# Reordering the end of a graph-attention kernel: the last pieces of k, two projection pieces, the statistics and the last row blocks' tiles

## Chip, cores, metric

One Trainium2 chip (trn2), one of its cores. The metric is the time of the whole kernel on the device in microseconds (us); lower is better. The kernel is already tuned: 3693 us long, TensorE busy for 99% of it.

## The reference, cut to what matters

Two layers on x of shape (32, 512, 512). The first is a graph convolution with residual and layer norm. The second is 8-head attention, masked by the adjacency matrix, again with residual and layer norm. There are 32 graphs (the kernel's *batches*) of 512 nodes with 512 features.

```
x = layernorm(x + deg * (x @ Wi.T + b) + adj @ (x @ Wj.T))
q, k, v = x @ Wq.T + bq, x @ Wk.T + bk, x @ Wv.T + bv          # 8 heads of 64
s = where(adj == 0, -inf, q k^T / 8)
x = layernorm(x + softmax(s) v @ Wo.T + bo)
```

## The kernel before: what the change touches

Batches are pipelined. While batch n does its attention in eight steps (scores, masked exponentials, values), TensorE is filled between the steps with *pieces* of other batches' projections: seven products per 512 x 512 block, named 1 to 7, each eight matmuls. `pj` is the output projection (pieces p1 to p7), `k` the key projection (k1 to k7). The last period has few pieces left, and that is where the change is. The list below is the last period; each inner list is one attention step of the last batch.

```
LATE = (5, 3, 6, 7, 4)
ALONE = ((1, "a"), (6, "b"), (2, "a"), (7, "b"), (5, "a"), (4, "b"), (3, "a"))

def phase_a(n):                      # the pieces at the end of a period
    A, K = banks(n)
    if n == B:
        return [pc("k", n - 1, i, bank) for i, bank in ((6, K), (5, A), (7, K), (3, A), (4, K))]
    ...

def last_steps():
    m = B - 2
    p = {i: pc("pj", m, i, bank) for i, bank in ALONE}
    c = [z(combos, TO, m, ot_quarter(m), (1, 2)), z(combos, TO, m, ot_quarter(m), (3, 4))]
    own = [(4 * GA, last_part, c, 0) for c in range(2)]
    return [[z(last_load), FLUSH, c[0], p[1], c[1]], [p[2], p[6]], [p[5], p[7], z(add_bo, B - 1, 0), z(add_bo, B - 1, 1)],
            [p[3], p[4], z(stats, m, 0), z(stats, m, 1)], [z(apply, m, 0), z(apply, m, 1), z(store, m)], [own[0]], [own[1]], []]
```

Words used below, with their lines in the kernel before: the *mask product* (VectorE, L495) multiplies the exponentials by the mask and so frees the scores' PSUM tile; *pre-sums* and *sums of weights* (L501 on GpSimd, L503 on VectorE) add up the weights of a row, and `sums` (L522) makes its *denominators* of them on TensorE; reciprocals (L531) and scalings (L547) turn values into the scaled output oT and so free the values' PSUM tiles `ov`; *combinations* (GpSimd, L405) are sums of blocks of oT that the seven products need, `add_bo` (GpSimd, L387) the additions of the output bias; a *final unit* is a pair of matmuls of the last batch's output projection (`last_part`, L735 and L736); *statistics* (L298) are those of the layer norm, and the ScalarE pass that follows them at the end is L743. A step is *bare* when no piece stands in it. `FLUSH` issues at once all that is left of `rest`. (In later kernels the line numbers are a few lower or higher.)

The loop that runs a step: scores first, then the values of the step before, at the start of a group of four also its denominators (`sums`) and what follows from them (`rest`: four reciprocals, two scalings, one check sum), then the pieces, with the pre-sums of the weights (`presum`) and the rest dealt out between them.

```
scores(b, 2 * g, kc); scores(b, 2 * g + 1, kc)
values(pb, pg, pk)
if pk == NC - 1:
    sums(pg, ...); drain(pb, pg); extra = rest(pb, pg)
late = [(presum, i, kc) for i in range(2) if kc > 0]
for f in PERIODS[n][step]:
    if f is FLUSH: some = len(extra)
    else:
        run(f)
        some = 0 if f[0] == 0.0 else len(extra) if step == 0 else max(1, round(f[0] / PC))
    if some:
        for g in late[:1] + extra[:some]: g[0](*g[1:])
        late, extra = late[1:], extra[some:]
for g in late + extra: g[0](*g[1:])
```

And the tail. `sc_tile()` gives a two-bank PSUM tile, of which there are two; `RL[g]` holds the denominators, as (PSUM tile, SBUF tile).

```
    else:
        t = sc_tile()
        ACC[2], ACC[3] = t[:, 0, :], t[:, 1, :]        # in last_part: two row blocks in one tile
...
for c in range(2):
    last_part(c, 1)
for ic in range(NC):
    c = slice(ic * P, (ic + 1) * P)
    invert(1, ic, 0)                                     # reciprocal straight from PSUM
    scale(B - 1, 1, 0, c); scale(B - 1, 1, 1, c)
    last_part(2, ic=ic); last_part(3, ic=ic)
    if ic > 0: last_rows(ic - 1)                         # BN statistics, ScalarE pass, store
tell_all(B - 1, 1)
last_rows(NC - 1)
flags()
```

## Time and profile before

| | before |
|---|---|
| time | 3696.01 us, median of 3 (3695.45 to 3696.68) |
| profiled execution | span 3693.0 us, granted clock 0.998 |
| TensorE busy | 3662.9 us, 99% |
| VectorE, GpSimd, ScalarE busy | 65%, 53%, 28% |

The page and the views that matter are shown in the prediction below. In a timeline line, read: start and length in us, engine, source line, operation, output <- input, number of instructions merged; in brackets the idle time before the line and what ended it. In a windows line: the stretch and its length; busy time and instructions of PE, PEld, DVE, ACT, POOL; then granted clock, DMA share, GB/s.

### The profile page before, as it was taken

What the parts mean: (1) busy time and instruction counts of PE and PEld (TensorE: products, weight loads), DVE (VectorE), ACT (ScalarE), POOL (GpSimd) and SP (SyncE); (2) the same over time, 40 slices, a digit from 0 to 9 for tenths busy, and PEclk for the clock granted to TensorE, in tenths of its full rate; (3) what the DMA queues carried; (4) which work ended last, traced back from release to release, by engine and by line L of the source; (5) the groups of instructions that cost most, each with busy time, mean ns of one, the idle gap of its engine ahead of it and who ended that gap; (6) DMA issues with size and microseconds to landing.
All of it is one profiled execution on the core that took longest, in us unless ns stands there. A gap on an engine that the chain in (4) does not pass through costs nothing.

```text
span 3693.0 us, 49640 instructions
## 1 busy us (share of the span) xinstructions
PE 3662.9 (99%) x18470; PEld 2510.3 (68%) x18470; DVE 2393.1 (65%) x3134; ACT 1028.6 (28%) x1483; POOL 1940.0 (53%) x1985
## 2 busy tenths in 40 slices
PE   9999999999999999999999999999999999999998
PEld 6766667676767676767676767676767666666663
DVE  4666666666666666666666666666666666666665
ACT  2232232222222223222223222223232322222322
POOL 3555545556445555455554555644555545555443
PEclk9999999999999999999999999999999999999999
DMA  8445556444555445564555544455545555445541
GB/s 258 141 120 140 138 154 160 139 131 135 151 157 151 129 135 146 152 165 125 135 140 151 162 144 128 136 150 155 158 123 138 142 158 159 134 133 139 148 138 44
DMA packets 797173, 530.02 MB, mean 144 GB/s; under 512 B 530432, under 2 KB 611840, under 8 KB 796928
## 3 DMA queue, kind: packets, MB, share of 16 engines
q1 hardware_dynamic: 780384, 494.78, 49.7%
q10 hardware_dynamic: 16320, 31.46, 2.3%
q8 instruction: 151, 2.47, 0.3%
q14 instruction: 94, 0.77, 0.1%
q0 software_dynamic: 224, 0.53, 0.0%
HBM read 453.25 MB, written 73.40 MB: 143 GB/s over the span
## 4 chain that ended last, share of the span: by engine, by line
PE 97%; DVE 1%; POOL 0%; DMA 0%; ACT 0%; SPq 0%; issue 0%; DVEq 0%; ACTq 0%; POOLq 0%
PE mma L436 31%; PE mmb L436 31%; PE sc L490 13%; PE ov L512 12%; PE mmb L334 4%; PE mma L334 3%; PE sc L522 2%; PE mmb L611 0%; PE mma L611 0%; DVE e L495 0%; DVE rl L531 0%; DMA xa<-hd 0%; SPq L376 0%; PE sc L736 0%; DVE st L298 0%
## 5 line engine op out<-in xcount | busy, mean ns | idle before, releaser
L494 ACT ACTIVATE sc<-sc 128x1024 f32<-128x1024 f32 x512 | 493.0, 1007 | 1554.8 <-PE sc L490 1548.8
L495 DVE TENSOR_TENSOR e<-sc,edge 128x1024 f32<-128x1024 f32 x512 | 602.6, 1218 | 205.8 <-ACT sc L494 173.3
L436 PE MATMUL mmb<-ring,big 128*128 128x256 f32 x3144 | 731.7, 381 | 0.0
L436 PE MATMUL mma<-ring,big 128*128 128x256 f32 x3112 | 724.4, 381 | 1.5 <-DVE xh L454 0.8
L436 PEld LDWEIGHTS mmb<-ring,big 128*128 128x128 f32 x3144 | 591.9, 190 | 131.6 <-issue 27.7
L436 PEld LDWEIGHTS mma<-ring,big 128*128 128x128 f32 x3112 | 585.8, 190 | 132.3 <-issue 26.5
L405 POOL TENSOR_TENSOR big<-big 128x512 f32<-128x512 f32 x376 | 492.4, 1339 | 34.5 <-DVE big L382 14.3
L490 PE MATMUL sc<-q,k 64*128 64x512 f32 x2048 | 509.4, 615 | 0.0
L512 PE MATMUL ov<-e,v 128*32 128x512 f32 x4096 | 492.4, 598 | 4.6 <-DVE oT L547 4.6
L501 POOL TENSOR_TENSOR es<-e 128x1024 f32<-128x1024 f32 x128 | 300.8, 2361 | 350.2 <-DVE e L495 350.2
L436 PE MATMUL mma<-big,ring 128*128 128x256 f32 x1808 | 430.3, 381 | 0.0
L436 PE MATMUL mmb<-big,ring 128*128 128x256 f32 x1776 | 422.8, 381 | 1.0 <-DVE v L465 1.0
L300 POOL TENSOR_SCALAR mv<-mv 128x1 f32<-128x1 f32 x256 | 49.8, 194 | 674.2 <-DVE mv L299 661.9
L436 PEld LDWEIGHTS mma<-big,ring 128*128 128x128 f32 x1808 | 340.5, 190 | 73.0 <-issue 26.0
L436 PEld LDWEIGHTS mmb<-big,ring 128*128 128x128 f32 x1776 | 334.3, 190 | 73.4 <-issue 26.0
L512 PEld LDWEIGHTS ov<-e,v 128*32 128x32 f32 x4096 | 106.9, 109 | 351.9 <-issue 320.8
L204 POOL TENSOR_TENSOR xlo<-xh,xhi 128x512 fp32r<-128x512 f32 x128 | 162.7, 1283 | 338.1 <-ACT xhi L203 338.1
L490 PEld LDWEIGHTS sc<-q,k 64*128 64x128 f32 x2048 | 176.3, 186 | 208.2 <-issue 207.0
L349 POOL TENSOR_TENSOR big<-big,deg_r 128x512 f32<-128x512 f32 x124 | 173.5, 1400 | 263.5 <-DVE big L348 263.5
L503 DVE TENSOR_TENSOR es<-es,e 128x1024 f32<-128x1024 f32 x250 | 304.8, 1220 | 0.0
L454 DVE TENSOR_TENSOR xh<-xh,mma 128x512 f32<-128x512 f32 x186 | 126.7, 681 | 263.9 <-PE mma L436 263.9
L454 DVE TENSOR_TENSOR xh<-xh,mmb 128x512 f32<-128x512 f32 x186 | 126.7, 681 | 259.2 <-PE mmb L436 259.2
(161 smaller groups left out, 3663.6 us busy)
## 6 DMA issues: line engine op xcount, KB each, us to landing
ring<-wo SPq DMA_DIRECT2D x217, 256.0 KB, 2.8
ring<-wq SPq DMA_DIRECT2D x160, 256.0 KB, 3.9
ring<-wv SPq DMA_DIRECT2D x160, 256.0 KB, 3.4
ring<-wk SPq DMA_DIRECT2D x160, 256.0 KB, 3.3
ring<-wi SPq DMA_DIRECT2D x155, 256.0 KB, 2.7
ring<-wj SPq DMA_DIRECT2D x155, 256.0 KB, 2.6
xh<-in_x_dram SPq DMA_DIRECT2D x32, 1024.0 KB, 5.4
xa<-in_x_dram SPq DMA_DIRECT2D x124, 256.0 KB, 4.0
```

The source lines that it names most:

```text
L204: nc.gpsimd.tensor_sub(lo, xs, hi.bitcast(FT))
L334: nc.tensor.matmul(pm, parts[w][:, jc, :], adjR[:, jc, :], start=(w == 0 and jc == 0), stop=(w == 1 and jc == NC - 1))
L349: nc.gpsimd.tensor_tensor(XD[b][:, dc, :], XD[b][:, dc, :], deg_r, op=OP.mult)
L405: nc.gpsimd.tensor_tensor(dst, p, q, op=OP.subtract)
L436: nc.tensor.matmul(pm[:, c * Q:(c + 1) * Q], lhs, rhs, start=first, stop=(kc == 1 and n == len(terms) - 1), skip_group_check=True)
L454: nc.vector.tensor_tensor(d, d, pm, op=OP.add)
L490: nc.tensor.matmul(ps[:, s, :], KT[b, hp // 2][r, hp % 2, kc * P:(kc + 1) * P], QT[b, hp // 2][r, hp % 2, :], start=True, stop=True)
L494: nc.scalar.activation(ps, ps, AF.Exp, scale=QSCALE)
L495: nc.vector.tensor_tensor(e, ps, edge[:, kc:kc + 1, :].to_broadcast([P, 2, N]), op=OP.mult)
L501: nc.gpsimd.tensor_add(ES[i], E[i, 0], E[i, 1])
L503: nc.vector.tensor_add(ES[i], ES[i], E[i, kc])
L512: nc.tensor.matmul(PV[g][r][32 * h:32 * h + 32, :], V[b][:, kc, c0:c0 + 32], E[h // 2, kc][:, h % 2, :], start=(kc == 0), stop=(kc == NC - 1))
```

## The change

Two of k's last five pieces go behind the last batch's first scores; p3 and p4 go behind the first denominators of the last batch; the statistics of the batch before come later still; the last two row blocks get a tile each; and the last denominators are drained into SBUF as all others are.

```diff
@@ phase_a
-            return [pc("k", n - 1, i, bank) for i, bank in ((6, K), (5, A), (7, K), (3, A), (4, K))]
+            return [pc("k", n - 1, i, bank) for i, bank in ((5, A), (6, K), (3, A))]
@@ last_steps
-        p = {i: pc("pj", m, i, bank) for i, bank in ALONE}
+        A, K = banks(B)
+        p = {i: pc("pj", m, i, K if i in (6, 7, 4) else A) for i in ORDER}
...
-        return [[z(last_load), FLUSH, c[0], p[1], c[1]], [p[2], p[6]], [p[5], p[7], z(add_bo, B - 1, 0), z(add_bo, B - 1, 1)],
-                [p[3], p[4], z(stats, m, 0), z(stats, m, 1)], [z(apply, m, 0), z(apply, m, 1), z(store, m)], [own[0]], [own[1]], []]
+        k = [pc("k", B - 1, i, K) for i in (7, 4)]
+        return [[z(last_load), k[0], FLUSH, c[0], p[1], c[1], k[1]], [p[2], p[6]], [p[5], p[7], z(add_bo, B - 1, 0), z(add_bo, B - 1, 1)],
+                [], [p[3], p[4]], [own[0], z(stats, m, 0), z(stats, m, 1)], [own[1], z(apply, m, 0), z(apply, m, 1), z(store, m)], []]
@@ last_part
-                t = sc_tile()
-                ACC[2], ACC[3] = t[:, 0, :], t[:, 1, :]
+                ACC[ic] = sc_tile()[:, 0, :]
@@ the tail
-    for c in range(2):
-        last_part(c, 1)
+    drain(B - 1, 1)
     for ic in range(NC):
         c = slice(ic * P, (ic + 1) * P)
-        invert(1, ic, 0)
+        invert(1, ic)
         scale(B - 1, 1, 0, c)
         scale(B - 1, 1, 1, c)
+        if ic < 2:
+            last_part(0, 1, ic + 2)
+            last_part(1, 1, ic + 2)
         last_part(2, ic=ic)
         last_part(3, ic=ic)
...
-    tell_all(B - 1, 1)
+    tell(B - 1, 1)
```

More of the change, by code (lines that the diff above doesn't have):

```diff
@@ L527, in drain, with invert @@
         nc.scalar.activation(RL[g][1], RL[g][0], AF.Identity, accum_out=told[:, j:j + 1])
-    def invert(g, part, src=1):
+    def invert(g, part):
         c = slice(part * P, (part + 1) * P)
-        nc.vector.reciprocal(RL[g][1][:, c], RL[g][src][:, c])
+        nc.vector.reciprocal(RL[g][1][:, c], RL[g][1][:, c])
     def tell(b, g):
@@ L535, in tell @@
         nc.vector.reduce_sum(told[:, j:j + 1], RL.pop(g)[1], axis=AX.X)
-    def tell_all(b, g):
-        pl, rl = RL.pop(g)
-        j = 2 * (b * 2 + g)
-        nc.gpsimd.memset(told[:, j + 1:j + 2], 0.0)
-        nc.vector.tensor_tensor_reduce(pl, pl, rl, 1.0, 0.0, OP.add, OP.add, told[:, j:j + 1])
     def scale(b, g, r, c=slice(0, N)):
@@ L568, in gnn_attention_kernel @@
     LATE = (5, 3, 6, 7, 4)
-    ALONE = ((1, "a"), (6, "b"), (2, "a"), (7, "b"), (5, "a"), (4, "b"), (3, "a"))
     def banks(n):
```

## The prediction

> **What bounds the kernel now.** I read the page first, then TensorE's timeline over the last 200 us, the windows with the granted clock, the chain of waits over the same stretch, and the timelines of VectorE and GpSimd beside it.
>
> ```profile
> PE 3662.9 (99%) x18470; PEld 2510.3 (68%) x18470; DVE 2393.1 (65%) x3134; ACT 1028.6 (28%) x1483; POOL 1940.0 (53%) x1985
> ```
>
> TensorE is busy for 99% of 3693.0 us; its idle time lies mostly in the first 15 us and in the end. The change keeps every matrix product (the built kernels have the same number of matmuls) and first departs from the kernel before at 3567 us. So only the last 126 us can change, and within them TensorE's gaps and the tail after its last product. The gaps (last bracket of a line: idle before it, and who ended it):
>
> ```profile
> 3571.61 1.92 PE L512 MATMUL ov<-e,v 128*32 128x512 f32 x16 [0.63 <-DVE oT L547]
> 3590.77 1.99 PE L436 MATMUL mmb<-big,ring 128*128 128x256 f32 x8 [0.98 <-DVE v L465]
> 3613.29 1.92 PE L512 MATMUL ov<-e,v 128*32 128x512 f32 x16 [1.18 <-DVE oT L547]
> 3639.74 1.50 PE L522 MATMUL sc<-es,ones 128*32 128x512 f32 x8 [2.00 <-DVE e L495]
> 3641.00 1.95 PE L522 MATMUL sc<-e,ones 128*32 128x512 f32 x8
> 3642.88 2.35 PE L490 MATMUL sc<-q,k 64*128 64x512 f32 x8
> 3647.96 1.92 PE L512 MATMUL ov<-e,v 128*32 128x512 f32 x16 [2.73 <-DVE oT L547]
> 3676.50 1.98 PE L736 MATMUL sc<-xh,oT 128*128 128x512 f32 x4 [0.46 <-DVE oT L547]
> 3678.69 1.98 PE L736 MATMUL sc<-xh,oT 128*128 128x512 f32 x4 [0.20 <-DVE oT L547]
> ```
>
> The two denominator lines (L522) last 1.50 and 1.95 us where the same eight take 1.04 elsewhere. The windows view says why: its clock column, after POOL's, falls to 0.56 just after the 2.00 us gap and is back at 1.00 four us later.
>
> ```profile
> 3638.00:3640.00 2.00, 0.26 (x4) 0.16 (x8) 1.97 (x4) 0.00 (x0) 1.63 (x5) 1.00 0.00 0
> 3640.00:3642.00 2.00, 2.00 (x16) 0.38 (x8) 0.82 (x1) 0.00 (x0) 1.02 (x4) 0.56 0.00 0
> 3642.00:3644.00 2.00, 2.00 (x12) 0.70 (x6) 0.28 (x1) 1.00 (x3) 0.00 (x0) 0.59 0.04 8
> 3644.00:3648.00 4.00, 1.26 (x10) 0.23 (x8) 3.90 (x6) 4.00 (x6) 0.00 (x0) 1.00 0.14 51
> ```
>
> The chain at the very end (start, us, what): the last statistics stand behind ScalarE's pass over the block before.
>
> ```profile
> 3680.71 0.71 DVE st L298
> ...
> 3682.94 0.78 ACT xh L743
> 3683.74 0.71 DVE st L298
> ...
> 3685.97 0.78 ACT xh L743
> ```
>
> The waits of the built code agree: that last BN-stats waits for ScalarE, because both blocks sit in one two-bank tile.
>
> **What the Trainium skill says.** "TensorE: Matmul & The Clock Gate", Part 1, has the clock fall to half after about one idle window of 3.4 us, and a window that runs freely. The trace agrees on the half rate (0.56) and the length, but 2.00 us of idle was enough; the 2.73 us gap brought none. "PSUM — Partial Sum Buffer", PSUM bank collisions, forbids two engines on one bank and allows different banks; the two halves of an sc tile are two banks, so separate tiles may drop that last wait. No collision shows here. "SBUF — State Buffer", Who interferes with whom, says a VectorE instruction with two SBUF inputs contends with GpSimd's reads. The trace agrees: the sums of weights (L503) take 1.22 us alone and 1.77 beside GpSimd's bias additions (L387).
>
> **The change, part by part.** I measure losses from start to start. Natural steps, from the timeline: a piece of eight products 1.73 us, 0.1 more beside a score step; scores 1.92; values 1.85; denominators 0.86 for eight; a final unit of two 0.86.
>
> *k's last pieces.* One piece fewer stands before the scores at 3569, so these start at 3567.26 and their values could at 3569.18. VectorE frees the old ov tiles: reciprocals from 3567.98 (four at 0.85, one already done) end at 3569.77, and values begin 0.74 after the first scaling starts, at 3570.52. Loss 1.34 instead of 0.70: +0.64. Next, the v piece and k piece that shared bank b back to back are parted by scores: the loss at 3590.77 (2.87 from start to start, less 1.73 = 1.14) goes. Three pieces, k7, p1, k4, now follow the denominators. From 3570.52 I add 1.86, two groups of 10.87 (four pieces, scores, values), 9.14 (three), 0.97, 5.38 and 1.92: values at 3611.5. The first scaling starts at 3606.1+0.65 (a k addition)+3.4 (reciprocals) = 3610.15, so they are free at 3610.9; the loss of 1.25 goes. Balance against 3613.29: -1.8.
>
> *The pieces p3 and p4 behind the denominators.* The kernel before has 12.93 from those values to the scores of the fourth step: 3624.43 now. Their values end at 3628.2, and nothing stands between them and the next scores, whose tile is free only after VectorE's mask product. That hangs on GpSimd: combinations from 3611.6, 7.39 to the presums, 4.69 to the second mask product, 5.65 to the first of the next pair: 3629.3, finished 3630.5. A **new wait** of 2.35 us, and 0.2 for the second half. Then values 3632.7, denominators 3634.5 (no statistics ahead of them: the 2.07 and the slow 1.42 go), p3 3636.25, p4 3638.1, scores 3639.9. VectorE: p4's addition at 3640.1, three reciprocals 2.6, scaling 3643.35, values at 3644.1. Loss 2.28 instead of 3.16. Against 3647.96: -3.9, if the clock holds.
>
> *Statistics after the next scores.* They leave the denominators' path, but GpSimd's twelve small operations (four times 1.27 us) now stand between its two presums. First presum 3646.45 to 3648.8; small ones to 3653.9; second presum to 3656.3. The mask product of the next step reuses the block that it reads, ends at 3657.5, and the second half of the last scores waits for it: 1.27 lost. At the first final unit: 3667.20-3.9+1.3 = 3664.6, -2.6.
>
> *Row blocks' tiles and denominators through SBUF.* The drain on ScalarE puts about 0.7 us ahead of the first reciprocal, but three units lie beside it: that reciprocal at 3665.4, its scaling usable at 3666.85, TensorE gets there at 3667.25. The fourth scaling, behind the second block's statistics as before, lets the last group begin at 3675.7 instead of 3678.69: -3.0. The 0.68 us reduction replaces a custom operation of 0.81. Last statistics: 2.02 after that group's start, 3677.7, against 3683.74. ScalarE no longer in front is a further -3.0. The tail from there is unchanged, the memset aside.
>
> Sum: -3.0 - 3.0 = -6.0 us, span 3687.0, time 3690.0. Then the clock. A half-rate window costs about 1.7 us. With gaps of 1.7 us harmless and 2.0 harmful, the free window catches the new 2.35 us gap in about half the runs and the 2.28 us one nearly so: an estimate of 1.5 us in the mean. **Prediction: 3691.5 us, -0.12%.**
>
> **Rivals.** (1) *The ends simply add, no new wait*: all six gaps vanish, 10 us, plus 3 at the tail: 3683. Against it: GpSimd's presums already hold a mask product for 4.08 us in this trace, and the pieces that covered it are moved. (2) *Bare steps starve TensorE twice*: scores, values, scores, values, denominators are light, both gaps fall to half clock, the late presum costs 2 us more: 3694 to 3697, no gain. For it: one 2 us gap did this before. (3) *The tail is set by something else* (the flag or the last store): then the last 3 us stay, 3693 to 3694.5. Against: the last ScalarE pass ends at 3686.75 and the span 6.25 later; the flag's last operation ends 0.8 before it, and in the new order the flag follows the same statistics, so all move together.
>
> **Range and chances.** Low 3687.5: no half-rate window and waits 2.5 us smaller than my walk. High 3696: rival 2 nearly whole, or a chip that sits a little higher; three runs before spread over 1.2 us. A gain or loss of 2% would be 74 us, half the stretch concerned: faster 0.003, slower 0.007, same 0.99.
>
> **What would show it.** Right: no idle before the products near 3590 and 3613; a new wait of about 2.3 us ahead of scores near 3630, ended by VectorE's e; about 2.3 us ahead of values near 3644, ended by oT; a GpSimd presum at about 3654, after small operations, and about 1.3 us before scores near 3657; the last statistics on VectorE ended by TensorE, not ScalarE; last final group at about 3676. Wrong: half clock in none or both places moves the end by 1.7 us each; a last wait on the flag or a store refutes the tail; movement before 3567 us would mean that something outside the diff differs.

## The result

| | before | after |
|---|---|---|
| median, lowest to highest, us | 3695.4, 3692.25 to 3696.68 (6 runs) | 3690.06, 3688.87 to 3691.26 (6 runs) |
| ratio, 95% interval | | 0.9987, 0.9974 to 1.0 |
| profiled span | 3693.0 | 3687.9 |

A ratio here is the mean time of one kernel's fast runs over the mean of the other's of the same rounds, so not quite the ratio of the medians quoted. The verdict at 2% is "same", as foreseen: 5.3 us of 3695. The time lies in the range; the middle was 1.4 us too high.

TensorE's timeline after, the lines with an idle time and, unbracketed, the values that follow the second of them (compare the nine lines of before in the prediction):

```profile
3570.41 1.92 PE L512 MATMUL ov<-e,v 128*32 128x512 f32 x16 [1.26 <-DVE oT L540]
...
3630.51 3.46 PE L490 MATMUL sc<-q,k 64*128 64x512 f32 x8 [2.42 <-DVE e L495]
3633.91 2.09 PE L512 MATMUL ov<-e,v 128*32 128x512 f32 x16
...
3645.35 1.92 PE L512 MATMUL ov<-e,v 128*32 128x512 f32 x16 [2.08 <-DVE oT L540]
...
3658.76 1.13 PE L490 MATMUL sc<-q,k 64*128 64x512 f32 x4 [1.10 <-DVE e L495]
...
3676.98 1.98 PE L730 MATMUL sc<-xh,oT 128*128 128x512 f32 x4 [0.46 <-DVE oT L540]
```

The waits near 3590 and 3613 are gone. The first has grown (1.26), a new one stands at 3630, the one for the scaled outputs has shrunk from 2.73 to 2.08, and half of the last scores waits 1.10. The scores at 3630 last 3.46 us where eight such matmuls take 1.99. The windows view after gives the reason, in its clock column (0.72, 0.50, 0.93):

```profile
3630.00:3632.00 2.00, 1.49 (x4) 0.59 (x6) 1.59 (x2) 0.00 (x0) 0.45 (x1) 0.72 0.00 0
3632.00:3634.00 2.00, 2.00 (x10) 0.44 (x10) 0.65 (x1) 1.01 (x1) 0.00 (x0) 0.50 0.00 0
3634.00:3636.00 2.00, 2.00 (x20) 0.59 (x24) 1.52 (x2) 1.01 (x1) 0.00 (x0) 0.93 0.00 0
...
3682.00:3684.00 2.00, 0.00 (x0) 0.00 (x0) 0.00 (x0) 0.00 (x1) 0.00 (x0) 0.52 0.43 132
```

(The last line lies behind the last product. It costs nothing, but dates the clock's windows further down.)

GpSimd's timeline after: its two pre-sums (L501), with twelve small operations between them, of which the first is shown.

```profile
3647.70 2.35 POOL L501 TENSOR_TENSOR es<-e 128x1024 f32<-128x1024 f32 x1 [17.25 <-DVE e L495]
3650.13 0.19 POOL L300 TENSOR_SCALAR mv<-mv 128x1 f32<-128x1 f32 x1
...
3655.09 2.35 POOL L501 TENSOR_TENSOR es<-e 128x1024 f32<-128x1024 f32 x1
```

VectorE's timeline after: the mask product that waited for that second pre-sum (TensorE's 1.10 us hang on it), and the last statistics, now released by TensorE and not by ScalarE.

```profile
3657.48 2.49 DVE L495 TENSOR_TENSOR e<-sc,edge 128x1024 f32<-128x1024 f32 x2 [3.13 <-POOL es L501]
...
3679.01 0.70 DVE L298 BATCH_NORM_STATS2 st<-sc 128x6 f32<-128x512 f32 x1 [0.49 <-PE sc L730]
```

**A common zero.** Single executions differ by more than these effects, before the change begins: the denominators of batch after batch keep nearly the same distances in the traces compared (58.2 and 55.2 us in turn; from the first of them to the *zero* defined next 3397.8 to 3398.5 us), but the first starts at 160.2 us in one and 164.2 in another, though the kernels are the same up to there. Most of the difference lies in the first microseconds: waits for the adjacency matrix, and products at half speed (the first four of 128x512, L193, last 2.07 us before and 1.21 in "pre-sums first"; the clock column shows 1.00 there all the same). So I measure within a trace, from the start of the last denominators (L522) ahead of the change, those of the first group of the last batch but one, called *zero* (3560.91 us before, 3560.81 after). The marks: the values that run in step 1 of the last period; the first values after the last batch's first denominators (those of step 4; they run in step 5); the first final unit; the last ScalarE pass. Each mark comes from one profiled execution per kernel. The expectations below call the zero "the seventh (batch's last) denominators" and the last batch "the eighth"; these are slips, their 105.15 us is counted from this zero. "Half" counts stretches of half clock before the last product.

| kernel | time, us | values step 1 | values step 4 | first final unit | last ScalarE pass | half |
|---|---|---|---|---|---|---|
| before | 3695.40 | 52.38 | 87.05 | 106.29 | 125.06 | 1 |
| after | 3690.06 | 50.51 | 84.54 | 105.15 | 120.42 | 1 |
| tail only | 3689.99 | 52.38 | 86.68 | 107.50 | 122.77 | 2 |
| order only | 3693.40 | 50.51 | 84.55 | 105.17 | 123.95 | 1 |
| k's pieces only | 3692.17 | 50.50 | 83.40 | 103.98 | 122.76 | 1 |
| after, statistics at once | 3693.51 | 50.51 | 87.98 | 108.85 | 124.13 | 2 |
| after, pre-sums first | 3689.14 | 50.50 | 84.59 | 104.28 | 119.54 | 1 |
| after, reciprocals first | 3689.62 | 50.51 | 82.41 | 103.74 | 119.01 | 1 |
| after, p1's additions first | 3686.23 | 50.50 | 81.33 | 101.95 | 117.21 | 0 |
| after, these three | 3684.21 | 50.50 | 79.20 | 99.62 | 114.88 | 0 |
| k's pieces and tail | 3689.64 | 50.51 | 83.40 | 104.28 | 119.55 | 1 |
| after, bias early | 3687.18 | 50.51 | 82.15 | 102.75 | 118.02 | 0 |
| after, p3 back | 3687.05 | 50.51 | 82.27 | 103.15 | 118.42 | 1 |
| after, four edits | 3683.84 | 50.51 | 78.26 | 98.69 | 113.96 | 0 |

Times are medians: six runs each for the first two rows, five for the others. The kernel before, run again beside the others, had medians of 3694.1, 3694.36 and 3693.62 us (9 runs in each of the three groups). Where two kernels differ by about a microsecond, only the marks tell them apart.

### The profile page after: what moved, and what is told of

Its sections match the earlier page's. It is cut to its first block, busy times and chain, and to the rows that moved or that the text cites. A ratio compares the mean times of both kernels' runs of the same rounds, so it can differ in the third digit from the quotient of the medians.

```text
span 3687.9 us, 49638 instructions
## 1 busy us (share of the span) xinstructions
PE 3662.2 (99%) x18470; PEld 2511.0 (68%) x18470; DVE 2393.1 (65%) x3133; ACT 1029.4 (28%) x1485; POOL 1939.0 (53%) x1984
## 4 chain that ended last, share of the span: by engine, by line
PE 98%; DVE 1%; POOL 1%; ACT 0%; issue 0%; DMA 0%; SPq 0%; DVEq 0%; POOLq 0%; ACTq 0%
PE mma L436 31%; PE mmb L436 31%; PE sc L490 13%; PE ov L512 13%; PE mmb L334 4%; PE mma L334 3%; PE sc L522 2%; PE mmb L604 0%; PE mma L604 0%; POOL es L501 0%; DVE e L495 0%; DVE rl L531 0%; PE sc L730 0%; DMA big<-in_adj_dram 0%; POOL big L405 0%
## 5 line engine op out<-in xcount | busy, mean ns | idle before, releaser
L501 POOL TENSOR_TENSOR es<-e 128x1024 f32<-128x1024 f32 x128 | 300.1, 2355 | 363.5 <-DVE e L495 363.5
```

The source lines that it names most:

```text
L501: nc.gpsimd.tensor_add(ES[i], E[i, 0], E[i, 1])
```

## The experiments

All gave the reference's result. My theory: the gain is a sum of separate waits, -1.8 (k's pieces), a small loss or gain from moving p3, p4 and the statistics, and -3.5 (tail). Rivals: the tail is set by something else; the reordering does everything; later waits absorb what earlier ones give.

### Tail only

The kernel before, with the last two parts of the diff (a tile for each row block, and the tail) alone.

> The kernel before with only the new tail: the last denominators drained by ScalarE into SBUF, a tile for each of the last two row blocks, their products in the new order. Theory (the tail is worth what its own chain shows, whatever comes before): 3.0 us because the last statistics no longer wait for ScalarE, 0.3 to 0.6 more from the order of the final units; 3.3 to 3.8 us faster than before, the two gaps near 3640 and 3648 unchanged. Rival (the tail gains only because TensorE arrives earlier, or the flag sets the end): under 1 us.

3689.99 us, ratio 0.999 (0.9976 to 1.0003). From the first final unit to the last ScalarE pass: 15.27 us (122.77 - 107.50) against 18.77 before (125.06 - 106.29): **-3.50**, with 15.27 in the changed kernel as well. VectorE's timeline of this run, its last statistics:

```profile
3679.66 0.70 DVE L298 BATCH_NORM_STATS2 st<-sc 128x6 f32<-128x512 f32 x1 [0.49 <-PE sc L735]
```

It waits for TensorE alone. That the tile of its own frees it, and not the drain or the new order in the same edit, is read from who ended the wait (ScalarE before, TensorE here); no run parts the three. From the start of the last final group to these statistics there are 2.02 us (3679.66 - 3677.64) against 5.05 before (3683.74 - 3678.69), so 3.0 of the 3.5 are the wait for ScalarE. The rival falls. The second gap is 2.37 us and not 2.73 as expected, because the scores ahead of it last longer at half clock (2.70 us, 2.35 before). This trace also caught two stretches of half clock, one more than before, which is why its first final unit comes later (107.50) though nothing ahead of it was touched. TensorE's timeline of this run, the second of them: values that take 3.50 us and not 1.92.

```profile
3645.80 3.50 PE L512 MATMUL ov<-e,v 128*32 128x512 f32 x16 [2.37 <-DVE oT L547]
```

### Order only

The kernel before, with `phase_a` and `last_steps` of the change alone.

> The kernel before with only the new order of pieces and statistics, the old tail. Theory (the parts add): what is left of the change after the tail, 1.2 us with one half-rate window as in the trace of after, 2.6 us without one; a new wait near 3630, a late second presum on GpSimd at about 3655. Rival (the order gives everything, the tail is hidden): 4 us or more. Rival (the order gives nothing, new waits eat all): within 0.5 us.

3693.40 us, ratio 0.9999 (0.9986 to 1.0013). First final unit at 105.17, **-1.12** against before, one stretch of half clock in both, and the three new waits as in the changed kernel (2.41, 2.08 and 1.11 us). Order -1.12 and tail -3.50 make -4.62; the changed kernel has -4.64 (125.06 - 120.42). The parts add.

### k's pieces only

```diff
-                [], [p[3], p[4]], [own[0], z(stats, m, 0), z(stats, m, 1)], [own[1], z(apply, m, 0), z(apply, m, 1), z(store, m)], []]
+                [p[3], p[4], z(stats, m, 0), z(stats, m, 1)], [z(apply, m, 0), z(apply, m, 1), z(store, m)], [own[0]], [own[1]], []]
```

(`last_steps` of the change with p3, p4 and the statistics where they had been; the tail of before.)

> The kernel before with only k's last two pieces moved behind the denominators; the projection's p3 and p4 and the statistics stay where they were. Theory: -1.8 us at the values near 3613 (the waits of 0.98 and 1.18 gone, the one near 3571 0.7 larger), carried to the end since the later waits hang on GpSimd and VectorE work that starts about 2 us earlier as well: 1.8 to 2.4 us faster. Rival (later waits absorb it, being fixed by other work): under 0.7 us at the end.

3692.17 us, ratio 0.9996 (0.9982 to 1.0009). Values of step 1 at 50.50 (-1.88), first final unit at 103.98: **-2.31**, and 1.19 us *earlier* than with the whole new order. So moving p3, p4 and the statistics costs 1.2 us in this pair of traces. TensorE's timeline of this run shows what it would have replaced:

```profile
3636.30 1.06 PE L522 MATMUL sc<-es,ones 128*32 128x512 f32 x8 [1.75 <-DVE e L495]
...
3643.26 3.28 PE L512 MATMUL ov<-e,v 128*32 128x512 f32 x16 [3.09 <-DVE oT L547]
```

Two waits, 4.84 us together, and one half-clock stretch; in the changed kernel three, 2.42, 2.08 and 1.10, 5.60 together, and one half-clock stretch. The move trades waits at a small loss.

### k's pieces and tail

The changed kernel with the same edit.

> The change without what its words name last: k's pieces and the tail as changed, but p3 and p4 ahead of the denominators and the statistics behind them as in the kernel before. Theory (from the two parts measured alone: -2.2 us for k's pieces, -3.5 for the tail, so p3, p4 and the statistics together cost 1.2 us): 104.0 us from the seventh denominators to the first final unit with one half-rate window, against 105.15 in the changed kernel, and 15.3 from there to the last ScalarE pass: 1 to 1.3 us faster than the changed kernel. Rival (the parts do not add: the move of p3 and p4 pays once the tail is new): 105.5 or more.

3689.64 us, ratio 0.9989 (0.9975 to 1.0003). First final unit at 104.28, 0.87 before the changed kernel's, and 15.27 from there. The theory holds, a little under its 1 to 1.3 us, since half clock cost more here than in the run before: from the values of step 4 to the next 9.05 us here and 8.75 there, 7.40 in the kernel before, where no half clock falls. Without these 1.65 and 1.35 us both first final units come at 102.63. The times (3689.64 and 3690.06, from different groups) don't tell the two kernels apart; the marks do, twice.

### Statistics at once

```diff
-                [], [p[3], p[4]], [own[0], z(stats, m, 0), z(stats, m, 1)], [own[1], ...
+                [], [p[3], p[4], z(stats, m, 0), z(stats, m, 1)], [own[0]], [own[1], ...
```

> The changed kernel with the statistics straight after p3 and p4, not after the next scores. Theory (the statistics' place matters through VectorE's queue): 3.2 us of them come ahead of the last three reciprocals, so the wait for the old sums near 3645 grows from 2.1 to about 5.2 us, while the second presum is no longer late and the 1.1 us wait near 3658 goes; 2 us slower than the changed kernel, more with a half-rate window after the long gap. Rival (TensorE has slack there): within 0.5 us of the changed kernel.

3693.51 us, ratio 1.0 (0.9986 to 1.0013). TensorE's timeline of this run:

```profile
3649.04 3.56 PE L512 MATMUL ov<-e,v 128*32 128x512 f32 x16 [5.25 <-DVE oT L540]
```

The wait of 5.25 came as worked out, with half clock behind it (3.56), and the wait near 3658 is gone. First final unit 3.7 later than in the changed kernel, not 2: the second stretch of half clock makes 1.6 of it (from the values of step 4 to the next 9.04 us against 7.41). Given that p3 and p4 go behind the denominators, the statistics had to move too.

### Pre-sums first

In the step of `own[0]`, both `presum`s are put ahead of the statistics.

```diff
-                ... [own[0], z(stats, m, 0), z(stats, m, 1)], ...
+                ... [own[0], SUMS, z(stats, m, 0), z(stats, m, 1)], ...      # SUMS: issue all pre-sums left, now
```

> The changed kernel with both presums of the last step but two put on GpSimd before the statistics' small operations. Distances are taken from the start of the seventh batch's last denominators to the first final unit, 105.15 us in the changed kernel, since the first microseconds differ from one execution to the next. Theory (the second presum is late because twelve small operations stand before it): the 1.1 us wait inside the last scores is gone, 104.0 us, all else as it was. Rival (the mask product waits for ScalarE's scores, not for the block that the presum reads): 105.1 us.

3689.14 us, ratio 0.9985 (0.9971 to 0.9999). First final unit at 104.28, -0.87: the 1.10 us wait is gone and 0.25 came up at the last denominators. The second pre-sum was late for its place in the queue.

### Reciprocals first

```diff
-                [], [p[3], p[4]], [
+                [], [FLUSH, p[3], p[4]], [              # FLUSH: reciprocals and scalings before the pieces
```

> The changed kernel with the four reciprocals and two scalings of the eighth batch's first half ahead of p3's and p4's additions in VectorE's queue. Theory (VectorE's reciprocals wait behind p4's addition, which waits for p4): the 2.1 us wait of the values near 3645 disappears or falls under 0.3, while the late second presum then costs up to 0.3 more; 103.0 to 103.4 us from the seventh denominators to the first final unit against 105.15. Rival (four reciprocals are 3.4 us whatever their place and set that wait): it stays above 1.5 us.

3689.62 us, ratio 0.9986 (0.9972 to 0.9999). The values of step 4 have no wait left, 2.13 us earlier (82.41). But the late pre-sum now holds the last scores 1.82 us instead of 1.10, more than I had allowed, so 1.41 us remain at the first final unit (103.74; I had expected 103.0 to 103.4). TensorE's timeline of this run, the two places:

```profile
3643.02 1.92 PE L512 MATMUL ov<-e,v 128*32 128x512 f32 x16
...
3657.15 1.13 PE L490 MATMUL sc<-q,k 64*128 64x512 f32 x4 [1.82 <-DVE e L495]
```

### p1's additions first

```diff
-        c = [z(combos, TO, m, ot_quarter(m), (1, 2)), z(combos, TO, m, ot_quarter(m), (3, 4))]
+        c = [z(combos, TO, m, ot_quarter(m), i) for i in ((1,), (2,), (3, 4))]
-        return [[..., FLUSH, c[0], p[1], c[1], k[1]],
+        return [[..., FLUSH, c[0], p[1], c[1], c[2], k[1]],
```

> The changed kernel with GpSimd's three additions of p1 (3.7 us) run before the second combination, in time in which GpSimd sat idle waiting for the scaled output. Theory (the new 2.4 us wait near 3630 hangs on GpSimd, whose presums start about 3.1 us too late): that wait gone or under 0.3 us, and with it in most executions the half-rate window; 102.7 us with a half-rate window elsewhere, 101.4 without, against 105.15. Rival (the wait is VectorE's own, two mask products and two sums in a row): it shrinks by under 0.8 us.

3686.23 us, ratio 0.9976 (0.9963 to 0.999). GpSimd's timeline of this run: the three additions (L451) start at 3608.70 and the pre-sums (L501) at 3616.08, which was 3618.88 in the changed kernel; from the common zero 55.01 against 58.07, 3.06 us earlier.

```profile
3608.70 3.73 POOL L451 TENSOR_TENSOR xh<-xh,p 128x512 f32<-128x512 f32 x3 [29.80 <-ACT p L443]
3612.39 1.28 POOL L405 TENSOR_TENSOR big<-oT,big 128x512 f32<-128x512 f32 x1
...
3616.08 4.69 POOL L501 TENSOR_TENSOR es<-e 128x1024 f32<-128x1024 f32 x2
```

TensorE's wait near 3630 falls to 0.58, and the clock stays at 1.00 there:

```profile
3628.93 2.26 PE L490 MATMUL sc<-q,k 64*128 64x512 f32 x8 [0.58 <-DVE e L495]
```

-3.20 us at the first final unit: 1.84 of wait (2.42 - 0.58) and 1.36 more. The latter is the half-clock stretch: from those scores to the denominators 3.93 us here, 5.31 in the changed kernel, 1.38 less. I had expected the wait below 0.3 and 101.4; it came 0.5 short. The rival, that VectorE alone makes the wait, falls.

### These three together

> The changed kernel with all three of these edits. Theory (three separate waits, and no half-rate window left when none of the gaps is near 2 us): 99.0 to 100.0 us from the seventh denominators to the first final unit against 105.15, so 5 to 6 us faster than the changed kernel and 9 to 11 faster than the one before, about 3684 us. Rival (the waits move rather than vanish, since VectorE is near full here): 2 to 3 us.

3684.21 us, ratio 0.9973 (0.9959 to 0.9987), 10.2 us below the median before of the same group. First final unit at 99.62, -5.53. TensorE's waits of this run up to the last final group:

```profile
3570.62 1.92 PE L512 MATMUL ov<-e,v 128*32 128x512 f32 x16 [1.26 <-DVE oT L540]
3628.90 2.26 PE L490 MATMUL sc<-q,k 64*128 64x512 f32 x8 [0.59 <-DVE e L495]
3656.22 1.06 PE L522 MATMUL sc<-es,ones 128*32 128x512 f32 x8 [0.98 <-DVE e L495]
3671.66 1.98 PE L731 MATMUL sc<-xh,oT 128*128 128x512 f32 x4 [0.45 <-DVE oT L540]
```

### Bias early

```diff
-        return [[z(last_load), k[0], ...], [p[2], p[6]], [p[5], p[7], z(add_bo, B - 1, 0), z(add_bo, B - 1, 1)],
+        return [[z(last_load), z(add_bo, B - 1, 0), z(add_bo, B - 1, 1), k[0], ...], [p[2], p[6]], [p[5], p[7]],
```

> The changed kernel with the four bias additions on GpSimd put ahead of the combinations, into its idle time near 3580 to 3610, so that they no longer run beside VectorE's sums of weights. Theory[...]: those two sums take 1.22 us each and not 1.76 and 1.69, the next mask products end 1.0 us earlier, the 2.4 us wait near 3630 falls to about 1.4 and brings no half-rate window: 102.8 us to the first final unit, 104.1 with a window, against 105.15. Rival (the sums are slow for another reason): they stay at 1.7 us and the wait at 2.4.

3687.18 us, ratio 0.9983 (0.9969 to 0.9996). VectorE's timeline, the two sums of weights, in the changed kernel:

```profile
3625.35 1.76 DVE L503 TENSOR_TENSOR es<-es,e 128x1024 f32<-128x1024 f32 x1
...
3627.63 1.69 DVE L503 TENSOR_TENSOR es<-es,e 128x1024 f32<-128x1024 f32 x1
```

and in this run:

```profile
3624.93 1.22 DVE L503 TENSOR_TENSOR es<-es,e 128x1024 f32<-128x1024 f32 x1
...
3626.67 1.22 DVE L503 TENSOR_TENSOR es<-es,e 128x1024 f32<-128x1024 f32 x1
```

They are 1.0 us shorter together, the wait near 3630 is 1.39 and not 2.42, no half clock follows, and the first final unit comes at 102.75 (-2.40), as expected.

### p3 back

```diff
-                [], [p[3], p[4]], [
+                [p[3]], [p[4]], [
```

> The changed kernel with p3 alone put back ahead of the denominators. Theory (the new wait near 3630 exists because nothing stands between two bare steps): p3's 1.8 us fill it, the rest of it 0.6, no half-rate window; in exchange the wait for the old sums near 3645 grows from 2.1 to about 2.9; 102.7 us to the first final unit, 104.1 with a window, against 105.15. Rival (the wait only moves, one for one): within 0.4 us of 105.15.

3687.05 us, ratio 0.9983 (0.997 to 0.9997). The wait near 3630 is 0.51 and the one near 3645 is 2.88, both as expected; half clock followed the second. First final unit at 103.15 (-2.00), a microsecond better than expected for a run with half clock: the wait of the last scores for the late pre-sum, 1.10 in the changed kernel, is not there. Putting a piece back between two bare steps helps; the rival of a wait that moves one for one falls.

### Four edits

The three edits and the early bias additions.

> The three edits together with the early bias additions as a fourth. Theory: what was left of the wait near 3630 (0.59 us) goes, the wait of 0.98 before the last denominators stays: 99.0 us to the first final unit against 99.6 with three edits and 105.15 in the changed kernel; about 3683.5 us. Rival (GpSimd's additions now delay something ahead of them): 99.6 or more.

3683.84 us (3683.34 to 3684.16), ratio 0.9973 (0.9959 to 0.9987). The wait near 3630 is gone, first final unit at 98.69, 0.93 less than with three edits. It beats both kernels: 9.8 us below the median before of the same group (3693.62).

## Why the prediction was right

- *Only the last 126 us can move.* Right: the profiled spans differ by 5.1 us, of which 0.10 lies ahead of zero, 4.64 between zero and the last ScalarE pass, and 0.36 behind it, where the prediction had no change.
- *k's last pieces, -1.8.* Right: -1.87 at the values of step 1 (52.38 to 50.51). First wait 1.33 us from start to start (3570.41 - 3567.16 - 1.92; said 1.34). Its "one already done" is a slip: two of the four reciprocals are done by 3567.98, and its 3569.77 is the end of the two left.
- *p3 and p4 behind the denominators: a new wait of 2.35 + 0.2, the next down to 2.28.* Right in size: 2.50 from start to start (3630.51 - 3626.16 - 1.85), and 2.14 (3645.35 - 3641.29 - 1.92). The cause given, GpSimd's place ahead of VectorE's mask products, was shown by "p1's additions first" and "bias early".
- *The late second pre-sum, 1.27.* Right: 1.28 from start to start (3658.76 - 3656.52 - 0.96); "pre-sums first" took it away.
- *Tail, -3.0 from ScalarE.* Right: 3.02, and the same in the tail-only run. Up to the last group the prediction had -3.0 without half clock; measured from zero it is -1.61 (117.78 to 116.17) with 1.38 us of half clock, and the order of the final units gave 0.47 of it (11.49 to 11.02 us). The tiles do what the Trainium skill's page "PSUM — Partial Sum Buffer" (PSUM bank collisions) allows for different banks: VectorE's last statistics (3679.01 to 3679.71) and ScalarE's pass over the block before (3679.25 to 3680.03) overlap, and the results are correct.
- *Half clock, 1.5 us in the mean.* Right in size and in kind; which of the two gaps would be hit was luck. It came after the 2.42 us gap, cost 1.38, and did not come after the 2.08 us gap. The clock column shows the freely running window that the prediction named. In the changed kernel half clock starts at 3630.88 (0.72 over 2 us is 1.12 us at half rate, at the end of that line) and again at 3682.08 (0.52): 51.20 us apart, 15.0 times 3.413. In the kernel before it starts at 3640.24 (0.56) and 3684.60 (0.65 from 3684 to 3686): 44.36 us, 13.0 times. So too in every trace with two stretches. Laying these windows over all 14 traces, from 3562 us to the last product, I summed the idle time inside each. All 12 stretches of half clock follow a window with at least 1.99 us of it (eleven with 1.99 to 2.45, one idle throughout); no window with 1.82 us or less is followed by one. The 2.42 us gap lay inside one window; a boundary cut the 2.08 us gap into 1.26 and 0.82, and the prediction's harmless 2.73 us gap into 1.82 and 0.91. A gap of 2.41 to 2.43 us was hit in five traces of five, one of 2.07 or 2.08 us near 3645 in none of five. With a limit of about 1.9 us and a random phase I would estimate 60% and 50%, close to the prediction's half each. Its "1.7 us harmless" has no line behind it; 1.75 us in one window was harmless later (k's pieces and tail).
- *The sum.* -6.0 without half clock, -4.5 with; measured -4.64 at the last ScalarE pass with one stretch in both kernels. The 3696.01 us from which the prediction subtracted had also been a high draw: six runs of the same kernel have a median of 3695.4, and three groups of nine later ones 3694.36, 3694.1 and 3693.62. These medians differ by more than the 1.4 us by which the time was missed, so that closeness is in part luck; the marks are the better test.
- *Rivals.* (1) No new wait: refuted by the line at 3630.51. (Its "six gaps, 10 us" is loose: the lines show seven, 8.18 us in all, and near 10 only with the products slowed by half clock.) (2) Bare steps eat the gain: partly right. Moving p3, p4 and the statistics costs 0.9 to 1.2 us by the marks, 1.1 with the half clock taken out of both sides, though not the whole gain. (3) The flag sets the tail: refuted by the tail-only run.

What the prediction did not see was that "keep p3 and p4 where they were" is a little better than the change; its own sums (+2.5 and +1.3 of new waits against 2.1, 1.4 and 0.9 saved) were too near to each other to say so.

## What to carry to other kernels

When an engine is 99% busy, walk its last gaps one by one, with the chain that releases each: here VectorE's and GpSimd's queues held it at four places, and small edits moved each. Work that is free to run anywhere belongs where its own engine is idle: GpSimd sat idle for 30 us and then did 3.7 us of additions in front of the chain that TensorE waited for. Filler taken from between two light steps leaves a hole there and may cost a stretch of half clock besides, and whether it does depends on how much of the hole falls into one window of the clock: about 2 of its 3.4 us were enough here. So look at the granted clock behind each hole, and compare marks inside traces when the start of an execution scatters more than the effect.

## What the Trainium skill lacked or had wrong

- "TensorE: Matmul & The Clock Gate" (Part 1) puts half clock after at least one idle window of about 3.4 us. Here a window that was idle for 1.99 to 2.45 of its 3.41 us was enough, 11 times in 11, and 1.82 us was not; where the limit lies between them, and whether it is idle time alone that counts, no run here shows. The page's freely running window is borne out (starts 15.0 and 13.0 windows apart), and so is the length of a stretch: in the changed kernel's three windows of 2 us the clock lacks 2 us times (0.28 + 0.50 + 0.07), 1.7 us, which at half rate is 3.4 us.
- "SBUF — State Buffer" (Who interferes with whom) calls the shared ports an exclusive lock, and the trace agrees; what it does not tell is how a trace shows the block: as a longer instruction, busy and not idle, on both sides in turn. In the changed kernel a GpSimd addition runs to 3626.03, the VectorE sum started at 3625.35 takes 1.76 us and not 1.22, the next addition, started at 3625.99, 2.26 us and not 1.27. Each ends about as if it had waited for the other (within 0.15 us), and so do the next two (1.69 and 2.24 us).
- No page that I read tells how far the first microseconds scatter: the first denominators, near 160 us, start at 160.2, 162.4, 162.8 and 164.2 us in four traces of programs equal up to there, the lowest and the highest of 14 among them.
